# Smaller first transfers, products that warm the array, one wider copy, and a respaced hand-over in an attention and expert kernel

## The chip, the cores and the metric

The kernel runs on one core of a Trainium2 chip. A core has five engines that work at the same time and wait for each other by semaphores: TensorE (PE, matrix products; its weight loads are a row of their own, PEld), VectorE (DVE), ScalarE (ACT), GpSimd (POOL) and SyncE (SP), which issues most transfers. Products are written to PSUM, a small memory in eight banks that PE, DVE and ACT reach; all else lies in SBUF, 128 partitions wide. Sixteen DMA engines carry the data between SBUF and the main memory (HBM). The metric is the time of one execution on the device, in microseconds.

## The reference

Two layers on an image batch `x` of shape (2, 256, 56, 56), seen as 2 × 3136 positions of 256 channels.

```python
# layer 0: a non-local block without softmax, per group of 16 channels
g_x, th_x, ph_x = (einsum('gdc,bcn->bgdn', w, xf) + b for w, b in ...)
f = einsum('bgdn,bgdm->bgnm', th_x, ph_x) / n
y = einsum('bgnm,bgdm->bgdn', f, g_x)
z = relu(batchnorm(w_out @ y + b_out) + x)

# layer 1: causal attention with 4 heads of 64, then 8 experts, two for each token
t = t + attention(layernorm(t))            # t: (2, 3136, 256)
probs = softmax(layernorm(t) @ gate_w + gate_b)
top2_vals, top2_idx = top_k(probs, 2)
out = sum over experts e of  weight_e * (gelu(xf @ w1_e + b1_e) @ w2_e + b2_e)
t = t + out
```

All of it is in float32. As layer 0 has no softmax, the product over positions can be folded: the kernel needs only the 256 × 256 Gram matrix of the rows of `x` and their sums.

## The kernel before, in words

**Layer 0.** The rows of both images are read into `xr` (L187), 128 positions to a row block, four blocks (512 KB) to a transfer, and the tail of 64 (L191). `gram` (L255) accumulates the Gram matrix of an image over 25 row blocks with two products each (257 and 129 columns, since only the upper part is needed). `fold` makes one 256 × 256 matrix of it and of the weights; `apply` (L324) multiplies the image with this matrix, adds, and takes the relu. The gram of the first image is the first work of PE. PE also needs `ident`, an identity matrix that GpSimd makes at the very start. This part is ordered by the scheduler of the language; from layer 1 on the order of the instructions on each engine is that of the program text (`manual_schedule`).

**Attention.** For each image, blocks of W = 448 queries (`i`, 0 to 6) and two pairs of heads (`hp`) run over key blocks of 128 (`j`). One step has three parts. `scores` multiplies keys and queries into a PSUM tile of two banks, one for each head of the pair (L653), ACT takes the exponential into an SBUF tile `st` (L661, five buffers), DVE masks it where it is cut by the diagonal (L663) and adds it to `acc`, from which the row sums come (L675). `values` multiplies `st` with the values three steps later (`LAG`) and accumulates in the PSUM tile `yp` (L693). `yp` has one buffer of two banks; each bank holds the products of one half of the keys of a block, so the result is the sum of the two banks. At the last key block ACT copies bank 0 into the query's place in `qT` (L703), and DVE adds bank 1 to it (L704); only then the first `values` of the next pair may write `yp`. At that first step the next `scores` stand ahead of `values` in PE's queue.

Then follow, spaced by a clock that counts steps (`later`, `due`): `sum_rows` (L720 to L731: row sums by PE, a copy by ACT, four small transfers to HBM and one back in another layout), `invert` (L740 to L746: the reciprocal on DVE, a transfer to HBM, two broadcasts back into `rb`), `scale` (L752: DVE multiplies `qT` with `rb`) and `hand_on`, which marks the queries as finished. `queue_of` sends the transfers of the very last pair through GpSimd's queue, all others through SyncE's.

**Work in between.** Between the steps run generators that are pulled piece by piece from a deque `queue`; a pull takes the first generator in it that has something to do (the value `True`), and goes on to the next where it says `False`. `tokens(b)` holds the output projection (L602, `project_out`, where `finished` allows it), the sort of tokens by expert (`dispatch`: many small DVE instructions and two PE products) and the scatter of rows to their slots in HBM, `x_slots` (L1284, GpSimd). For image 0 all of this takes place during the attention of image 1; at its end the rows of the first three expert blocks are read into `early_rows` (L1659). For image 1 it takes place among the expert blocks.

**Experts.** `experts` runs over 102 blocks `n` of 128 slots each (the loop begins at n = −1). A block has `hidden` (L1403), `inputs` and `weights` of the block two ahead (transposes L1380; a DVE copy of the expert's weights, L1391), `outputs` of the block three back (L1422; DVE adds the bias, L1432; written to `y_slots`, L1437), and then `between()`, which is `meanwhile`: it pulls two pieces, or three while the rows of image 1 are scattered. Rows come in groups of three blocks by `fetch` (L1329); group 0 is `early_rows`. At the front of `queue` stands `closing`: while the last pair of image 1 isn't finished, it moves the clock by 4, calls `due`, and yields twice, so one of `sum_rows`, `invert`, `scale` and `hand_on` comes with each block. Once `hand_on` has run, `tokens(1)` goes on with the last projections, the sort and the scatter. At last come the gathers of the outputs, the sums and the stores (`finish`).

Of the kernel before, what the change touches and what calls it, by code (L numbers as in the profile page):

```python
# [9 lines left out]
F32 = mybir.dt.float32  # L10
# [3 lines left out]
ALU = mybir.AluOpType  # L14
# [13 lines left out]
def conv_attn_moe_kernel(  # L28
# [51 lines left out]
    nc = tc.nc  # L80
    P = 128
    B, C, N = x.shape
# [21 lines left out]
    MIXED = MOST0 + E  # L104
    NBLK = (2 * B * N + E * (P - 1)) // P
    GB = 3

    MAIN = NBLK - GB
    SCALE = 1.0 / HS**0.5
# [63 lines left out]
    with tc.tile_pool(name="c_w", bufs=1) as cw, tc.tile_pool(name="c_s", bufs=2) as cs, tc.tile_pool(  # L173
# [9 lines left out]
        whole = N // P  # L183
        for b in range(B):
            nc.gpsimd.memset(xr[b][:, :, C : C + 1], 1.0)
            for n in range(0, whole, 4):
                nc.sync.dma_start(  # L187
                    out=xr[b][:, n : n + 4, :C],
                    in_=x_rows[b, n * P : (n + 4) * P].rearrange("(n p) c -> p n c", p=P),
                )  # L190
            nc.sync.dma_start(out=xr[b][: N - whole * P, whole, :C], in_=x_rows[b, whole * P :])  # L191
        for b in range(B):
# [124 lines left out]
        def apply(b, meanwhile):  # L317
# [22 lines left out]
                    waiting = n + m  # L340
            nc.sync.dma_start(out=kept[b], in_=ts[b][:, :, :C])

        folded = {}
        first = fold(0, gram(0, iter(())))
        second = fold(1, gram(1, first))
# [97 lines left out]
    def layer1(nm, general):  # L443

        with ExitStack() as whole:
# [170 lines left out]
            def attend(  # L616
# [63 lines left out]
                def values(n):  # L680
                    i, hp, j, first, last, order = steps[n]
                    k = chunk(j)
                    c0 = max(0, j * P - i * W)
                    sn = f"{nm}{b}_{hp}_{i}"
                    st = sts.pop(n)
                    if first:
                        yps[hp, i] = py.tile([P, 2, 512], F32, tag="y", name=f"yp_{sn}")
                    yp = yps[hp, i]

                    for h in range(0, k, HS):  # L690
                        end = last or (h and all(chunk(o) <= h for o in order[order.index(j) + 1 :]))
                        for a in range(2):
                            nc.tensor.matmul(  # L693
                                yp[a * HS : (a + 1) * HS, h // HS, c0:W],
                                v[hp][h : h + HS, j, a, :HS],
                                st[h : h + HS, a, c0:],
                                start=first,
                                stop=bool(end),
                            )
                    if last:  # L700

                        yh = qT[:, hp, i * W : (i + 1) * W]
                        nc.scalar.copy(yh, yp[:, 0, :W])  # L703
                        nc.vector.tensor_tensor(yh, yh, yp[:, 1, :W], ALU.add)  # L704
                        del yps[hp, i]
                        later.append((clock[0], sum_rows, hp, i, yh))

                def queue_of(hp, i):

                    return nc.gpsimd if (b, hp, i) == (B - 1, NH - 1, NB - 1) else nc.sync  # L710

                def sum_rows(hp, i, yh):
                    r = (b * NH + hp) * NB + i
                    sn = f"{nm}{b}_{hp}_{i}"
                    acc = accs.pop((hp, i))
                    sp = bank(f"sp_{b}_{hp}_{i}")

                    flat = acc.rearrange("p a w -> p (a w)")
                    for g in range(4):
                        nc.tensor.matmul(  # L720
                            sp[g * 32 : (g + 1) * 32, : W // 2], ones[:, :32],
                            flat[:, g * W // 2 : (g + 1) * W // 2], start=True, stop=True,
                        )
                    line = fs.tile([P, W], F32, tag="rb", bufs=3, name=f"line_{sn}")
                    nc.scalar.copy(line[:, : W // 2], sp[:, : W // 2])
                    halves = sum_d[r].rearrange("a (h w) -> (a h) w", h=2)
                    for g in range(4):
                        queue_of(hp, i).dma_start(
                            out=halves[g : g + 1], in_=line[g * 32 : g * 32 + 1, : W // 2]
                        )  # L730
                    queue_of(hp, i).dma_start(  # L731
                        out=sums[:, r], in_=sum_d[r].rearrange("a (p f) -> (a p) f", p=HS)
                    )
                    later.append((clock[0] + 4, invert, hp, i, yh))

                def invert(hp, i, yh):
                    r = (b * NH + hp) * NB + i
                    sn = f"{nm}{b}_{hp}_{i}"
                    back = fs.tile([P, 2 * W // P], F32, tag="back", name=f"back_{sn}")
                    nc.vector.reciprocal(back, sums[:, r])  # L740
                    queue_of(hp, i).dma_start(
                        out=inv_d[r].rearrange("a (p f) -> (a p) f", p=HS), in_=back
                    )
                    rb = fs.tile([P, W], F32, tag="rb", bufs=3, name=f"rb_{sn}")
                    for a in range(2):
                        queue_of(hp, i).dma_start(  # L746
                            out=rb[a * HS : (a + 1) * HS], in_=inv_d[r, a].partition_broadcast(HS)
                        )
                    later.append((clock[0] + 4, lambda hp, i, yh: scale(hp, i, yh, rb), hp, i, yh))
# [551 lines left out]
            def experts(w1s, w2s, b2s, ex, es, ps6, between, need, written):  # L1301
# [4 lines left out]
                def fetch(g):  # L1306
                    s, e = g * GB, (g + 1) * GB
                    b = 0 if e <= FULL0 else 1
                    need(b)
                    if g == 0:  # L1310
                        return early_rows, None
                    f = known[b][0]
                    xb = ex.tile([P, GB, xds[b].shape[1]], F32, tag="xb", bufs=3, name=f"xb_{nm}_{g}")
                    if b:
# [59 lines left out]
                def inputs(n, group):  # L1374
                    xb, to = group
                    g = n % GB
                    rows = xb[g] if n < GB else xb[:, g, :C]
                    tp = ps6.tile([P, 512], F32, tag="tp", bufs=2, name=f"tp_{nm}_{n}")
                    for c in range(NH):
                        nc.tensor.transpose(  # L1380
# [257 lines left out]
            def tokens(b, qT, done):  # L1638
# [5 lines left out]
                if b == 0:  # L1644
# [8 lines left out]

                    while not read[B - 1]:
                        yield False
                    for n in range(0, GB, 2):
                        m = min(2, GB - n)
                        xb = bg.tile([P, 2, C], F32, tag="xn", name=f"xb_{nm}_first{n}")
                        nc.sync.dma_start(  # L1659
                            out=xb[:, :m],  # L1660
                            in_=xds[0][n * P : (n + m) * P].rearrange("(n p) w -> p n w", p=P),
# [108 lines left out]
            def closing():  # L1770

                if not general:
                    while finished[B - 1][NH - 1] < N:
                        clock[0] += 4
                        due(clock[0])
                        yield True
                        yield True
                    while not projected[B - 1]:
                        yield False
                    queue.append(judge())  # L1780
# [5 lines left out]
            with ExitStack() as moe:  # L1786
# [11 lines left out]
                        )  # L1798
                for _ in load_w2(True):
                    pass  # L1800
                while len(early_rows) < GB:
                    pull()

                def need(b):
# [9 lines left out]
                    queue.appendleft(finish(1, oy, 3))  # L1814

                def meanwhile():
                    scatters = placed[1] and not sent[1]
                    pull(3 if scatters or worked[0] >= MIXED else 2)
                    if side and next(side[0], None) is None:
                        side.popleft()  # L1820

# [179 lines left out]
```

## Time and profile before

The median of three runs is 1307.98 us (1307.3 to 1308.54). The profiled execution took 1332.96 us, with a span of 1331.2 us and a mean clock of PE of 0.989.

| | us |
|---|---|
| first product of PE (rows of the first image) | 6.19 |
| gram of image 0 done (copy out of PSUM) | 25.66 |
| attention, image 0 and 1 | 110.7 to 886.4 |
| first expert block | 888.2 |
| last projections of image 1 (L602) | 904.0 to 915.8 |
| sort of image 1 (L970 to L1138) | 921.2 to 963.1 |
| scatter of image 1 (L1284) | to 1042.6 |
| last store issued | 1323.9 |

| engine | busy, us | share |
|---|---|---|
| PE | 1276.9 | 96% |
| PEld | 808.0 | 61% |
| DVE | 787.7 | 59% |
| ACT | 602.2 | 45% |
| POOL | 306.2 | 23% |

How to read the rows of the profile below: a row of waits has the engine and line that waited, what ended the wait, then the total in us, the number of times and the longest. A row of the timeline has the start and the length in us, the engine, the line, the operation, what is written and read, the shape, the number of instructions merged in it, and in brackets the idle time of the engine ahead of it with what ended it. A row of a stretch has its bounds, its length, then busy time and number of instructions of PE, PEld, DVE, ACT and POOL, the clock granted to PE, the mean share of the DMA engines, and GB/s. A product in float32 shows as two records.

### The profile page before, as it was taken

The numbers are of one execution on the slowest core, as the hardware profiler recorded it, in microseconds if no ns is written. First come the engines' busy times: TensorE is split into PE (matmuls) and PEld (weight loads), VectorE is DVE, ScalarE is ACT, GpSimd is POOL, SyncE is SP. The second block draws the span as 40 slices with busy tenths as digits, with TensorE's granted clock in tenths as the row PEclk, the third lists the DMA queues.
The fourth block names the chain that finished last, engine by engine and source line by source line (L and its number), as shares of the span: only waits on it lengthen the run. The fifth ranks groups of instructions, "written<-read, shape, count | busy, mean of one in ns | idle before, by whom it ended". The sixth has DMA issues, their size and how long they took to land.

```text
span 1331.2 us, 28014 instructions
## 1 busy us (share of the span) xinstructions
PE 1276.9 (96%) x10569; PEld 808.0 (61%) x10569; DVE 787.7 (59%) x1683; ACT 602.2 (45%) x1226; POOL 306.2 (23%) x297
## 2 busy tenths in 40 slices
PE   8999999999999999999999989989999999899995
PEld 7875444444444444444345434449988999899894
DVE  1582555748777654675768777765744443355553
ACT  0145554555565554455553455553423333244341
POOL 1113110000000111110004461010066212655541
PEclk9999999999999999999999999999999999999997
DMA  9993000000000000100001126141244433556553
GB/s 311 383 326 113 16 24 24 24 16 24 9 17 17 17 2 9 40 9 15 9 8 60 60 80 198 33 138 56 67 144 129 130 109 97 179 175 202 180 156 107
DMA packets 110471, 123.54 MB, mean 93 GB/s; under 512 B 19904, under 2 KB 100045, under 8 KB 110329
## 3 DMA queue, kind: packets, MB, share of 16 engines
q1 hardware_dynamic: 96232, 92.49, 22.4%
q0 software_dynamic: 10272, 26.00, 5.8%
q10 hardware_dynamic: 3824, 3.18, 0.8%
q8 instruction: 87, 1.43, 0.5%
q14 instruction: 56, 0.45, 0.1%
HBM read 62.65 MB, written 60.41 MB: 92 GB/s over the span
## 4 chain that ended last, share of the span: by engine, by line
PE 91%; DVE 3%; issue 2%; ACT 1%; DMA 1%; POOL 0%; DVEq 0%; SPq 0%; POOLq 0%; ACTq 0%
PE yp_f L693 20%; PE sc_f L653 19%; PE ht_f L1403 14%; PE yp_f L1422 13%; PE qk_f L539 7%; PE v_f L558 4%; PE pp_f L602 4%; PE cp L324 3%; PE gram L255 3%; PE tp_f L1380 2%; DVE acc_f L675 1%; ACT st_f L661 1%; PE sp_f L720 1%; PE yo_f L1549 1%; PE xp_f L518 1%
## 5 line engine op out<-in xcount | busy, mean ns | idle before, releaser
L661 ACT ACTIVATE st_f<-sc_f 128x896 f32<-128x896 f32 (+5 forms) x400 | 333.5, 838 | 300.1 <-PE sc_f L653 273.7
L675 DVE TENSOR_TENSOR acc_f<-acc_f,st_f 128x896 f32<-128x896 f32 (+5 forms) x372 | 366.5, 985 | 168.3 <-ACT st_f L661 161.3
L693 PE MATMUL yp_f<-st_f,v_f 64*64 64x448 f32 (+6 forms) x3184 | 340.5, 503 | 9.7 <-DVE qT_f L704 6.5
L653 PE MATMUL sc_f<-qT_f,kT_f 64*64 64x448 f32 (+6 forms) x3184 | 341.5, 500 | 4.0 <-ACT st_f L661 4.0
L1412 ACT ACTIVATE g_f<-ht_f,b1b 128x128 f32<-128x128 f32 x408 | 116.8, 371 | 243.0 <-PE ht_f L1403 127.6
L1403 PE MATMUL ht_f<-xT_f,w_f 128*128 128x128 f32 x1632 | 203.4, 277 | 9.3 <-issue 6.6
L653 PEld LDWEIGHTS sc_f<-qT_f,kT_f 64*64 64x64 f32 x3184 | 116.6, 133 | 156.4 <-issue 134.5
L693 PEld LDWEIGHTS yp_f<-st_f,v_f 64*64 64x64 f32 x3184 | 112.3, 133 | 162.6 <-issue 134.7
L1403 PEld LDWEIGHTS ht_f<-xT_f,w_f 128*128 128x128 f32 x1632 | 198.5, 193 | 14.9 <-issue 10.4
L501 POOL TENSOR_SCALAR xn_f<-t 128x256 f32<-128x256 f32 (+1 forms) x50 | 68.2, 1373 | 542.6 <-issue 330.8
L1284 POOL DMA_INDIRECT x_slots<-xr_f,idx x100 | 113.0, 1130 | 218.7 <-DVE xr_f L1276 116.6
L1391 DVE COPY w_f<-w1s_f 128x1024 f32 x102 | 71.1, 698 | 86.8 <-PE ht_f L1403 38.8
L539 PE MATMUL qk_f<-px_f,wat 128*128 128x512 f32 (+1 forms) x224 | 92.6, 558 | 1.2 <-ACT px_f L524 1.2
L1439 POOL DMA_INDIRECT y_tokens<-ys_f,to_f x60 | 60.3, 1005 | 139.7 <-DVE ys_f L1432 109.8
L1432 DVE TENSOR_TENSOR ys_f<-yp_f,kT_f 128x128 f32<-128x128 f32 x102 | 29.6, 291 | 99.7 <-PE yp_f L1422 65.3
L663 DVE TENSOR_TENSOR st_f<-st_f,keep 128x256 f32<-128x256 f32 (+1 forms) x112 | 44.2, 395 | 68.2 <-ACT st_f L661 67.7
L539 PEld LDWEIGHTS qk_f<-px_f,wat 128*128 128x128 f32 x224 | 38.7, 190 | 54.4 <-issue 45.3
L1422 PE MATMUL yp_f<-px_f,g_f 128*128 x204 | 62.7, 390 | 1.0 <-issue 1.0
L1422 PE MATMUL yp_f<-v_f,g_f 128*128 x204 | 61.5, 382 | 0.8 <-issue 0.8
L1422 PE MATMUL yp_f<-kT_f,g_f 128*128 x204 | 62.1, 386 | 0.0
L1422 PE MATMUL yp_f<-w2s_f,g_f 128*128 x204 | 61.2, 382 | 0.3 <-issue 0.3
L1496 POOL DMA_INDIRECT y_f<-y_slots,idx x50 | 54.8, 1096 | 16.3 <-issue 14.7
(259 smaller groups left out, 1170.8 us busy)
## 6 DMA issues: line engine op xcount, KB each, us to landing
x_slots<-fill SPq DMA_DIRECT2D x1, 8127.0 KB
xb_f<-x_slots SPq DMA_DIRECT2D x60, 129.0 KB
x_slots<-fill SPq DMA_DIRECT2D x1, 7296.0 KB
y_slots<-ys_f SPq DMA_DIRECT2D x57, 128.0 KB
kept<-t SPq DMA_DIRECT2D x2, 3200.0 KB
x<-in_x_dram SPq DMA_DIRECT2D x14, 448.0 KB
xr<-in_x_rows_dram SPq DMA_DIRECT2D x12, 512.0 KB
out_dram<-ot_f SPq DMA_DIRECT2D x24, 256.0 KB
```

Source lines behind the costliest of these rows:

```text
L501: nc.gpsimd.tensor_scalar(xn[:k, a], ts[b][:k, n + a, :C], ts[b][:k, n + a, MEAN : MEAN + 1], ts[b][:k, n + a, RSTD : RSTD + 1], ALU.subtr ...
L539: nc.tensor.matmul(ps[:, :w], wat[:, c, d0 : d0 + P], xT[:, c, :w], start=(c == 0), stop=(c == NH - 1),)
L653: nc.tensor.matmul(ps[h : h + HS, a, c0:W], kT[hp][rows, j * P + h : j * P + h + HS], qT[rows, hp, q0 + c0 : q0 + W], start=True, stop=True,)
L661: nc.scalar.activation(st[:k, :, c0:], ps[:k, :, c0:W], AF.Exp, scale=SCALE)
L675: nc.vector.tensor_tensor(acc[:k, :, c0:], acc[:k, :, c0:], st[:k, :, c0:], ALU.add)
L693: nc.tensor.matmul(yp[a * HS : (a + 1) * HS, h // HS, c0:W], v[hp][h : h + HS, j, a, :HS], st[h : h + HS, a, c0:], start=first, stop=bool( ...
L1284: s = nc.gpsimd.indirect_dma_start(out=xds[b], out_offset=bass.IndirectOffsetOnAxis(ap=idxs[b][:kk, k, n : n + 1], axis=0), in_=xr[:kk], i ...
L1391: nc.vector.tensor_copy(w, w1s[:, :, bass.ds(e, 1), :].rearrange("p c e h -> p c (e h)"))
L1403: nc.tensor.matmul(ht[:, k, :], w[:, c, k * P : (k + 1) * P], xT[:, c, :], start=(c == 0), stop=(c == NH - 1),)
L1412: nc.scalar.activation(g[:, k, :], ht[:, k, :], AF.Gelu, bias=b1bs[b][:, k, i : i + 1])
L1422: nc.tensor.matmul(yp[:, :C], g[:, k, :], w2s[k][:, bass.ds(e, 1), :].rearrange("p e d -> p (e d)"), start=(k == 0), stop=(k == KH - 1),)
L1439: s = nc.gpsimd.indirect_dma_start(out=y_tokens, out_offset=bass.IndirectOffsetOnAxis(ap=to[:, n % GB : n % GB + 1], axis=0), in_=ys, in_o ...
```

## The change

Six edits, each at a place where the kernel goes from one stage to the next.

- The first four row blocks of image 0 come in transfers of one, one and two blocks, so that the first is small.
- Fourteen products of the identity with itself, whose result nobody reads, stand ahead of the gram on PE: they keep the array at work while the rows are on their way.
- At the end of a pair, ACT copies both banks of `yp` in one instruction into a tile from the score buffers, and GpSimd adds the halves: `yp` is free after one copy.
- The last row sums go through SyncE's queue like the others (`queue_of` goes).
- The rows of the first six expert blocks, two groups, are read early.
- `closing` gives six and then four pieces of room after its first two steps, then none; and three pieces are pulled in each block from the end of the projections of image 1 on, not only from the scatter on.

```diff
+    EARLY = 2
...
-            for n in range(0, whole, 4):
+            starts = [0] * (b > 0) + [0, 1, 2] * (b == 0) + list(range(4, whole, 4)) + [whole]
+            for n, end in zip(starts, starts[1:]):
...
+        idle = cbig.tile([P, P], F32, tag="big", name="idle")
+        for _ in range(14):
+            nc.tensor.matmul(idle, ident, ident, start=True, stop=True)
         folded = {}
         first = fold(0, gram(0, iter(())))
...
-                        nc.scalar.copy(yh, yp[:, 0, :W])
-                        nc.vector.tensor_tensor(yh, yh, yp[:, 1, :W], ALU.add)
+                        both = fst.tile([P, 2, W], F32, tag="st", name=f"both_{sn}")
+                        nc.scalar.copy(both, yp[:, :, :W])
+                        nc.gpsimd.tensor_tensor(yh, both[:, 0], both[:, 1], ALU.add)
...
-                    return nc.gpsimd if (b, hp, i) == (B - 1, NH - 1, NB - 1) else nc.sync
...
-                        queue_of(hp, i).dma_start(
+                        nc.sync.dma_start(
...
-                    if g == 0:
-                        return early_rows, None
+                    if g < EARLY:
+                        return early_rows[s:e], None
...
-                    rows = xb[g] if n < GB else xb[:, g, :C]
+                    rows = xb[g] if n < EARLY * GB else xb[:, g, :C]
...
-                    for n in range(0, GB, 2):
-                        m = min(2, GB - n)
-                        xb = bg.tile([P, 2, C], F32, tag="xn", name=f"xb_{nm}_first{n}")
+                    for n, m in ((0, 2), (2, 2), (4, 1), (5, 1)):
+                        name = f"xb_{nm}_first{n}"
+                        if m == 2:
+                            xb = bg.tile([P, 2, C], F32, tag="xn", name=name)
+                        else:
+                            xb = bg.tile([P, C], F32, tag="xr", name=name).unsqueeze(1)
...
+                    blocks = deque((3, 2))
                     while finished[B - 1][NH - 1] < N:
                         clock[0] += 4
                         due(clock[0])
-                        yield True
-                        yield True
+                        for _ in range(2 * blocks.popleft() if blocks else 0):
+                            yield True
...
-                while len(early_rows) < GB:
+                while len(early_rows) < EARLY * GB:
...
-                    scatters = placed[1] and not sent[1]
-                    pull(3 if scatters or worked[0] >= MIXED else 2)
+                    sorting = projected[1] and not sent[1]
+                    pull(3 if sorting or worked[0] >= MIXED else 2)
```

## The prediction

> **What bounds the kernel now.** I began with the chain that ended last and the waits of TensorE (PE), then looked at the three places the change touches.
>
> ```profile
> PE 91%; DVE 3%; issue 2%; ACT 1%; DMA 1%; POOL 0%; DVEq 0%; SPq 0%; POOLq 0%; ACTq 0%
> ```
>
> The end is set by PE: 91% of the chain is PE, which is busy for 1276.9 of 1331.2 us. An edit can shorten the kernel only by taking away time in which PE waits or runs slowly, and costs something only where it makes PE wait.
>
> The start, PE alone, in three stretches (busy time and number of PE products, then loads, DVE, ACT, POOL, clock, DMA share, GB/s):
>
> ```profile
> PE gram L255 <- DMA xr<-in_x_rows_dram: 6.2, 1, 6.2
> ...
> 6.10:12.00 5.90, 5.81 (x18) 4.99 (x19) 0.65 (x2) 0.90 (x1) 0.00 (x0) 1.00 1.03 350
> 12.00:18.00 6.00, 6.00 (x38) 5.49 (x37) 3.03 (x4) 0.89 (x2) 0.00 (x0) 1.00 1.10 336
> ```
>
> The first product waits 6.2 us for rows. Then PE does 18 products in 5.9 us, and 38 in the next 6.0: half speed at first, although the clock column reads 1.00 (single starts show it too: a 129-column product follows the one before after 0.215 us until 11.9 us, after 0.110 us from then on).
>
> PE's waits in attention, and one of them in order of time:
>
> ```profile
> PE yp_f L693 <- DVE qT_f L704: 6.5, 6, 1.5
> PE sc_f L653 <- ACT st_f L661: 4.0, 3, 1.5
> PE yp_f L693 <- issue: 1.4, 1, 1.4
> ...
> 197.25 0.53 ACT L703 COPY qT_f<-yp_f 128x448 f32<-128x448 f32 x1
> ...
> 198.39 0.62 DVE L752 TENSOR_TENSOR qT_f<-qT_f,rb_f 128x448 f32<-128x448 f32 x1
> 198.92 0.61 DVE L704 TENSOR_TENSOR qT_f<-qT_f,yp_f 128x448 f32<-128x448 f32 x1
> ...
> 199.59 0.21 PEld L693 LDWEIGHTS yp_f<-st_f,v_f 64*64 64x64 f32 x8 [1.80 <-DVE qT_f L704]
> 199.59 0.98 PE L693 MATMUL yp_f<-st_f,v_f 64*64 64x448 f32 x8 [1.02 <-DVE qT_f L704]
> ```
>
> The value tile has one buffer. It is free only when DVE has added the second bank (L704), and DVE takes that add after other work: ACT's copy was done at 197.78, the add began at 198.92. Seven of the 27 hand-overs hold PE so, for 6.5 + 1.4 = 7.9 us (the one marked "issue" is at 778.8, where the add ended at 778.76).
>
> The passage from attention to the experts:
>
> ```profile
> DVE back_f L740 <- DMA sums<-sums: 6.5, 1, 6.5
> DVE qT_f L752 <- DMA rb_f<-inverses: 5.2, 1, 5.2
> ...
> PE ht_f L1403 <- DVE w_f L1391: 2.7, 1, 2.7
> PE tp_f L1380 <- DMA xb_f<-x_slots: 1.1, 1, 1.1
> ...
> 893.20:898.50 5.30, 2.41 (x20) 2.21 (x20) 0.88 (x2) 2.04 (x8) 1.07 (x2) 1.00 0.09 21
> 898.50:905.50 7.00, 6.96 (x33) 6.46 (x34) 1.93 (x4) 1.41 (x5) 1.14 (x3) 0.76 0.10 33
> ```
>
> Block 3's rows come 1.1 us late. Then the reciprocal of the last row sums (L740) stands 6.5 us at the head of DVE's queue; the weight copy behind it (L1391) is late, and PE waits 2.7 us for it. Afterwards the clock is 0.76 for 7 us.
>
> **What the Trainium skill says.** *TensorE: Matmul & The Clock Gate*, Part 1: the array starts at half clock and is let go after a busy window of about 3.4 us; the window runs freely, so it takes 3.4 to 6.8 us. The trace agrees (5.7 us). *SBUF — State Buffer*, "Who interferes with whom": a DVE instruction with two SBUF inputs contends with a GpSimd one that reads SBUF; the trace before has no such pair that I could time. *GPSIMD Engine Reference*, 3.1: a two-input add of 2048 fp32 takes 4497 ns, used below.
>
> **Start: small transfers and idle products.** The identity is ready at 1.80 us. Each fp32 product shows as two records, so 14 products are 28. At half speed a record of this size takes 0.215 us, at full 0.110. Starting at 1.9 and let go after 5.7 us, as in this trace, at 7.6, PE has done 26.5 records; the rest takes 0.2, so gram begins at 7.8 at full speed. A block of rows then costs 0.657 us (0.220 + 0.216 + 0.110 + 0.111), 25 of them 16.4: gram ends at 24.2 instead of 25.6, a gain of 1.4. Bounds: let go after 3.4 us, gram starts at 6.6 and ends at 23.1 (gain 2.5); after 6.8, the idle products end at 7.9, gram's first 0.8 us are slow, and it ends at 24.7 (gain 0.9). The rows must keep up: by the packets of their queue the second to fifth transfers of 512 KB had landed by 8.5, 11.3, 13.6 and 16.1 us; the moved gram wants them at 10.4, 13.0, 15.7 and 18.3 (four blocks, 2.6 us, each), so there are 1.7 us in hand. But a transfer waits for the completion of one issued some eight earlier (the third issue stood until 5.78, for a weight load), so small transfers use up places. I take **1.4**, from 0.3 to 2.5. The transfers alone would be worth more than they show here, as PE is held by the idle products until 7.8 anyway.
>
> **One copy for both value banks.** It removes the DVE add from the release (27 × 0.62 us of DVE) and makes the copy 896 columns wide. The exponential of 128x896 takes 0.918 us; of 128x512 0.597, a copy of 128x512 0.586; so the copy should take about 0.91, which is 0.38 more for ACT (45% busy). The tile is then free 0.97 us after the copy's start. For the seven waits I compare this with when PE would have gone on, 0.37 us after its last group of score products: 131.13 against 130.82 and 516.52 against 516.22 leave 0.3 each; 198.22 against 198.40, 586.80 against 586.99, and the three others leave nothing. Gain 7.9 − 0.6 = **7.3**, from 5 to 7.9. The longer copy delays the next exponential by 0.38; its values are wanted three steps of about 1.5 us later, so no PE wait.
> The add moves to GpSimd. By the skill's price it takes 448/2048 × 4497 = 0.98 us (an estimate); by the nearest row (L501, 128x256 in 1.37 us) 2.4. I take 1.5. It is wanted only at L752, after a round trip through memory; but it holds one of the five score buffers, which the exponential four steps (6 us) later takes. Ahead of it in GpSimd's queue stand at most two or three scatters of 1.13 us: 3.4 + 2.4 = 5.8 us at worst. Cost 0.
>
> **The passage.** The early rows of blocks 3 to 5 are read during attention, which takes out the 1.1 us wait; group 2's fetch is due only at block 6. The last sums go through SyncE: earlier ones took 854.12 to 856.23 for the four rows, and inverses to broadcast 861.86 to 864.21, so 2 to 2.4 us a leg; on GpSimd the four issues took 2.6, and the landing another 3.8 us. Spacing counts most: each block pulls two pieces of work, so the reciprocal moves from block 0 to block 2 and the scaling from block 1 to block 4. Sums leave ACT at 888.7, so they are back at about 893.5, behind 1 MB of weights; DVE reaches the reciprocal at about 895. Inverses leave at 895.5, are back by 900.5, and DVE reaches the scaling after block 4's hidden products, about 901. Neither should stand at the head of DVE for long. Behind them on DVE are the weight copies, which PE wants two blocks later. Gain: 1.1 + 2.7 + 7.0 × 0.24 = 5.5 us, from which I take off 0.4 for a short rest of a wait: **5.1**, from 2 to 5.5. SyncE queues the writes of the expert outputs behind these waits; the first is needed only three blocks later.
> One cost I can't see: the new tile lies in memory that expert tiles take over, so the first weight copy may wait for GpSimd's add, between 0 and 1.7 us. I take 0.3.
>
> **Three pieces a block while sorting.** DVE was busy 30.6 of 43 us from 921 to 964; 14.6 of that is weights and outputs, 16 sorting. Half as much more sorting per block makes 3.4 of 3.73 us. Full, but the weight copies have two blocks in hand. Cost 0, and no gain: PE has no wait where the sort's result is first needed, near 1043 us.
>
> **Sum.** 1.4 + 7.3 + 5.1 − 0.3 = 13.5 us, so 1307.98 − 13.5 = **1294.5**. (The profiled execution is 23 us longer than the timed ones; PE waits marked "issue" near 995, 1023, 1144 and 1164 may be part of this. The waits counted here have a releaser in the program, so I carry them over in full.)
>
> **Rivals.**
> B, *the waits in attention come back*: a longer ACT copy or a late GpSimd add holds exponentials up, and nothing of the 7.3 remains: 1308 − 6.2 = 1301.8. For it: PE already waits 4.0 us for exponentials (L653). Against: these are three waits only, and ACT has half its time free.
> C, *the passage's wait only moves*: the scaling stands on DVE for its broadcast at block 4, or the tile taken over delays block 0: of 5.1 some 1.5 stays: 1308 − 1.4 − 7.3 − 1.5 = 1297.8. For it: three legs in memory lie in four short blocks.
> D, *slower*: GpSimd and DVE contend for SBUF and a score buffer comes free late, at each of 27 ends by 0.45 us (12 us), while the fuller DVE makes the passage no better: 1308 − 1.4 + 12 = 1318.6. For it: DVE's main work here (L675) reads two SBUF operands; DVE's lag is what held PE before. Against: 17 us leave DVE.
>
> **Chances.** Forecast 0.60, B 0.15, C 0.15, D 0.10. Faster by over 0.2% takes in the first three, less a little for a mixture near zero: 0.87; same 0.03; slower 0.10. Range: the most of every gain is 2.5 + 7.9 + 5.5 = 15.9, and DVE's freed time may take a few smaller waits along: low 1289. Upward it takes in C and B: high 1303.
>
> **What the next profile shows.** Right: gram's products at one pace from about 7.8 us; the waits of L693 gone or under 1 us; clock near 1 at 890 to 910, no long DVE wait at L740. Wrong, if PE waits for exponentials (L653) longer than 4 us in all, if exponentials wait for GpSimd, or if PE waits for L1391 again.

## The result, and the profile after

The changed kernel takes **1302.59 us** (median of 4 runs, 1302.21 to 1305.95), the kernel before 1308.26 (4 runs, 1307.3 to 1309.54): a ratio of 0.9962, with an interval of 0.9943 to 0.998. So it is faster, by 5.7 us where 13.5 were forecast.

In the first profile of before, from which the prediction was made, and in e1 to e4, e14, e15 and the runs of before beside them, the experts took some 25 us more whatever the kernel, for a reason that stays open, so sizes are compared in the other runs alone, where before takes 1307 to 1308 us; its profile there is called *before, third profile*. Single profiles scatter by a microsecond or two besides.

The table adds up the span of three profiles, between marks that are the start of an instruction in the trace. The last column is a kernel of the experiments (e16, with the start of before), explained there. Sums can be off by 0.1 through rounding.

| us | before, third profile | after | e16 |
|---|---|---|---|
| to the first score product | 110.4 | 111.1 | 109.3 |
| attention, first to last score product | 768.3 | 764.8 | 760.9 |
| last score product to expert block 10 | 46.3 | 41.8 | 41.8 |
| block 10 to the last store's issue | 372.8 | 375.0 | 374.4 |
| last store's issue to the end | 7.5 | 8.2 | 8.6 |
| span | 1305.3 | 1301.0 | 1295.0 |

The gain of after lies in attention (3.5) and in the passage (4.5). The start, the later blocks and the end give 3.6 back. The chain that ended last is still PE's; its share fell from 91% to 88%:

```profile
PE 88%; DVE 3%; issue 2%; DMA 2%; ACT 2%; POOL 2%; DVEq 0%; POOLq 0%; SPq 0%; ACTq 0%
```

POOL, at 0% before, now has 2%, and the next views show where. (DMA has 2% in the third profile of before too.)

**The start.** The two largest waits of PE in the first 30 us, after:

```profile
PE idle L349 <- POOL ident masks.py:199: 1.9, 1, 1.9
PE gram L258 <- DMA xr<-in_x_rows_dram: 1.9, 1, 1.9
```

And two stretches of it, all engines (first pair: PE's busy time and products):

```profile
6.10:12.00 5.90, 5.90 (x39) 5.51 (x39) 0.26 (x2) 0.00 (x0) 0.00 (x0) 1.00 1.04 364
12.00:18.00 6.00, 4.14 (x26) 3.61 (x26) 3.42 (x5) 1.79 (x2) 0.00 (x0) 1.00 1.11 335
```

Before, PE did 18 products in the first of these stretches and 38 in the second; now 39 and 26, of which ten are idle products. By 18 us the gram is no further than before (53 of its records begun, 54 before). The array is warm when the rows come (the gram begins at 7.3 us, at full pace), but it then overtakes them: from 12.5 to 14.6 us it waits for the transfer that holds row blocks 8 to 11. The semaphore of that transfer counts sixteen completions; in the trace the first came at 11.3 us and the last at 14.6.

**Attention.** The largest waits of PE in attention, first before (third profile, 110 to 879 us), then after (110 to 876 us):

```profile
PE yp_f L693 <- DVE qT_f L704: 7.9, 7, 1.5
```

```profile
PE xp_f L525 <- POOL xn_f L508: 2.2, 2, 1.2
PE yp_f L700 <- DVE st_f L670: 1.5, 3, 1.1
PE sc_f L660 <- ACT st_f L668: 0.9, 2, 0.6
PE yp_f L700 <- ACT both_f L711: 0.9, 2, 0.4
```

The wait for DVE's add of the second bank is gone, and 0.9 us for the wide copy is what remains of it. New at the top stands a wait for rows that GpSimd normalises. Its place, first on POOL, then on PE:

```profile
447.38 1.25 POOL L712 TENSOR_TENSOR qT_f<-both_f 128x448 f32<-128x448 f32 x1 [39.14 <-ACT both_f L711]
448.61 8.88 POOL L508 TENSOR_SCALAR xn_f<-t 128x256 f32<-128x256 f32 x6
```

```profile
453.69 0.44 PE L525 MATMUL xp_f<-ident,xn_f 128*128 128x128 f32 x2 [1.16 <-POOL xn_f L508]
455.13 0.44 PE L525 MATMUL xp_f<-ident,xn_f 128*128 128x128 f32 x2 [1.01 <-POOL xn_f L508]
```

GpSimd stood for 39 us at the add of a pair (L712), whose banks were not there yet. The normalisations of image 1's first rows (L508) are behind it in the queue and start only at 448.61; PE then takes the rows as fast as they are made, 1.4 us apiece. The experiments show when GpSimd made them otherwise.

A second place is near 778 us, while GpSimd also scatters rows (all engines, the lines that matter):

```profile
776.52 0.97 POOL L1288 DMA_INDIRECT x_slots<-xr_f,idx  x1 [0.30 <-issue]
...
776.89 3.93 DVE L682 TENSOR_TENSOR acc_f<-acc_f,st_f 128x896 f32<-128x896 f32 x2
...
777.51 1.15 POOL L712 TENSOR_TENSOR qT_f<-both_f 128x448 f32<-128x448 f32 x1
...
778.70 1.73 ACT L668 ACTIVATE st_f<-sc_f 128x896 f32<-128x896 f32 x2 [3.20 <-POOL qT_f L712]
...
779.66 0.98 PE L660 MATMUL sc_f<-qT_f,kT_f 64*64 64x448 f32 x8 [0.65 <-ACT st_f L668]
```

The banks had been copied by 773.41. Three scatters go first, the add begins at 777.51, the exponential that follows it at 778.70 (ACT had been free for it from 775.50, 2.1 us after the copy), and PE's score products wait 0.65 us. The first of DVE's two adds (L682) beside it took 2.73 us instead of 1.09.

**The passage.** Stretches of the kernel after; PE's clock is the third number from the end:

```profile
888.00:893.50 5.50, 5.50 (x41) 5.19 (x40) 1.97 (x4) 2.58 (x10) 0.00 (x0) 1.00 0.43 125
893.50:900.50 7.00, 7.00 (x42) 6.23 (x41) 4.03 (x12) 1.86 (x7) 0.00 (x0) 1.00 0.09 29
```

The clock is 1.00 in both, where before had 0.76 in the second. PE has no wait in either: 41 products in the first 5.5 us, where before had 20 in 5.3. On DVE the reciprocal and the scaling no longer hold anything up:

```profile
887.42 0.20 DVE L744 RECIPROCAL back_f<-sums 128x7 f32<-128x7 f32 x1
...
894.90 0.62 DVE L756 TENSOR_TENSOR qT_f<-qT_f,rb_f 128x448 f32<-128x448 f32 x1
```

Neither has an idle time in brackets; before they stood 6.5 and 5.2 us at the head of DVE.

### The profile page after: what moved, and what is told of

The parts are those of the page before. It is cut to its first block, busy times and chain, and to the rows that moved or that the text cites. A ratio compares the mean times of both kernels' runs of the same rounds, so it can differ in the third digit from the quotient of the medians.

```text
span 1301.0 us, 28091 instructions
## 1 busy us (share of the span) xinstructions
PE 1269.3 (98%) x10597; PEld 806.6 (62%) x10597; DVE 792.0 (61%) x1655; ACT 610.7 (47%) x1226; POOL 343.6 (26%) x317
## 4 chain that ended last, share of the span: by engine, by line
PE 88%; DVE 3%; issue 2%; DMA 2%; ACT 2%; POOL 2%; DVEq 0%; POOLq 0%; SPq 0%; ACTq 0%
PE yp_f L700 20%; PE sc_f L660 19%; PE ht_f L1407 13%; PE yp_f L1426 12%; PE qk_f L546 7%; PE v_f L565 4%; PE pp_f L609 3%; PE cp L327 3%; PE gram L258 2%; PE tp_f L1384 2%; DMA xr<-in_x_rows_dram 1%; PE sp_f L724 1%; DMA y_tokens<-ys_f,to_f 1%; ACT st_f L668 1%; PE yo_f L1553 1%
## 5 line engine op out<-in xcount | busy, mean ns | idle before, releaser
L682 DVE TENSOR_TENSOR acc_f<-acc_f,st_f 128x896 f32<-128x896 f32 (+5 forms) x372 | 375.2, 1009 | 156.3 <-ACT st_f L668 147.3
L1407 PE MATMUL ht_f<-xT_f,w_f 128*128 128x128 f32 x1632 | 199.5, 275 | 0.6 <-ACT xT_f L1388 0.6
L712 POOL TENSOR_TENSOR qT_f<-both_f 128x448 f32<-128x448 f32 x28 | 36.3, 1296 | 522.7 <-ACT both_f L711 522.7
L508 POOL TENSOR_SCALAR xn_f<-t 128x256 f32<-128x256 f32 (+1 forms) x50 | 72.9, 1466 | 143.1 <-DVE t L171 48.7
L546 PEld LDWEIGHTS qk_f<-px_f,wat 128*128 128x128 f32 x224 | 38.7, 190 | 54.0 <-issue 43.6
```

The costliest lines, as they stand in the source:

```text
L508: nc.gpsimd.tensor_scalar(xn[:k, a], ts[b][:k, n + a, :C], ts[b][:k, n + a, MEAN : MEAN + 1], ts[b][:k, n + a, RSTD : RSTD + 1], ALU.subtr ...
L546: nc.tensor.matmul(ps[:, :w], wat[:, c, d0 : d0 + P], xT[:, c, :w], start=(c == 0), stop=(c == NH - 1),)
L682: nc.vector.tensor_tensor(acc[:k, :, c0:], acc[:k, :, c0:], st[:k, :, c0:], ALU.add)
L1407: nc.tensor.matmul(ht[:, k, :], w[:, c, k * P : (k + 1) * P], xT[:, c, :], start=(c == 0), stop=(c == NH - 1),)
```

## The experiments

Times are medians; each ratio is to before, measured beside the kernel. Line numbers shift by a few from kernel to kernel; the tile names stay. Parts are named as in the prediction: *start* (small transfers and idle products), *copy* (one copy, the add on GpSimd), *passage* (SyncE for the last sums, six early blocks, spaced pieces, fuller sorting).

**The parts one by one: e1 to e4.** The kernel before once more, and before with one part each.

```diff
# e2: one copy for both banks
-                        nc.scalar.copy(yh, yp[:, 0, :W])
-                        nc.vector.tensor_tensor(yh, yh, yp[:, 1, :W], ALU.add)
+                        both = fst.tile([P, 2, W], F32, tag="st", name=f"both_{sn}")
+                        nc.scalar.copy(both, yp[:, :, :W])
+                        nc.gpsimd.tensor_tensor(yh, both[:, 0], both[:, 1], ALU.add)
# e3: the passage alone
+    EARLY = 2
...
+                    blocks = deque((3, 2))
...
+                    sorting = projected[1] and not sent[1]
# e4: the start alone
+        for _ in range(14):
+            nc.tensor.matmul(idle, ident, ident, start=True, stop=True)
```

> The kernel before, unchanged. Its first profile had a span of 1331.2 us beside timed runs near 1308. Theory P (that profile is of an unusual execution): a second profile has a span near 1306, lacks the waits of TensorE marked issue near 993 to 1025 and 1143 to 1166 (18 us), and some of the waits in attention are smaller too. Theory R (a profile always makes this kernel 23 us slower): the second span is again near 1330. Time the same as before, within 0.1% under both.

> Of the change, only the one copy for both value banks with GpSimd's add. By the prediction's term it gains 7.3 us (seven waits of 7.9 us go, 0.6 stays): 1301.0. Rival: in timed executions these waits are smaller than in the first profile, and the gain is 2 to 4 us: 1304 to 1306.

> Of the change, only the passage from attention to the experts: six early row blocks, the last sums through SyncE, the spaced closing, three pieces a block from the end of the projections. By the prediction's term it gains 5.1 us: 1303.2; the waits of TensorE at the first expert blocks (1.1 and 2.7 us) and the low clock after them go. Rival: part of the gain is given back later, and it gains 2 us or less: 1306 or more.

> Of the change, only the small first transfers and the fourteen products of the identity. Prediction's term: a gain of 1.4 us, 1306.9. Theory S, from the profile after: the third transfer of four blocks is issued late, the gram waits 2 us for it, and there is no gain (0 to 0.6 us slower): 1308.3 to 1308.9.

Before took 1333.73 us beside these (51 runs). e1: 1335.4, ratio 1.0006 (0.9987 to 1.0024); e2: 1331.37, 0.9985 (0.997 to 1.0001); e3: 1334.59, 1.0013 (0.9997 to 1.0029); e4: 1334.95, 1.0008 (0.9991 to 1.0026). **Inconclusive**, because of what stands in the profile of e1 among the experts (two of the waits of PE from 905 us on, then a stretch of 100 us):

```profile
PE ht_f L1403 <- issue: 6.7, 9, 1.1
PE yp_f L1422 <- issue: 2.3, 4, 1.0
```

```profile
950.00:1050.00 100.00, 93.79 (x603) 85.48 (x603) 49.03 (x188) 32.05 (x115) 52.16 (x50) 0.95 0.41 129
```

The same stretch in the third profile of before:

```profile
950.00:1050.00 100.00, 100.00 (x695) 93.28 (x694) 55.07 (x195) 36.72 (x131) 53.47 (x50) 1.00 0.43 141
```

PE does 603 products instead of 695: it waits up to 1.1 us for nothing that the profile shows, and the mean clock of the stretch is 0.95. All four profiles here have such waits at L1403 and its like, before and its parts alike, so the kernel's edits don't make them; what does is open. The prediction left open whether such waits are part of the 23 us between profile and times. They are. They also swallow gains: in e3 block 5 began at 901.1 us, 8.5 earlier than in e1 (909.6), yet the ends differ by 2.7.

**Two mends, beside the changed kernel: e5 to e8.** e6 leaves the small transfers out and keeps the idle products; e7 puts the add on VectorE; e8 does both.

```diff
# e6, e8
-            starts = [0] * (b > 0) + [0, 1, 2] * (b == 0) + list(range(4, whole, 4)) + [whole]
-            for n, end in zip(starts, starts[1:]):
+            for n in range(0, whole, 4):
# e7, e8
-                        nc.gpsimd.tensor_tensor(yh, both[:, 0], both[:, 1], ALU.add)
+                        nc.vector.tensor_tensor(yh, both[:, 0], both[:, 1], ALU.add)
```

> The changed kernel, unchanged. In its first profile TensorE has no waits marked issue among the experts, while four other profiles (the kernel before and parts of the change) have 17 to 22 us of them, in stretches where products come in pairs 0.71 us apart. Theory H (these belong to the chip or the execution, not to the kernel): on a chip where the kernel before takes about 1333, this one has them too, and takes 1322 to 1330; on a chip where the kernel before takes about 1308, it takes about 1302.6 without them. Theory K (the change itself removes them): it takes 1301 to 1306 wherever it runs.

> The changed kernel with the first rows in transfers of 512 KB as before; the idle products stay. Theory S (the small transfers use up places in the queue, so that the third transfer of four blocks is late and the gram stands 2.1 us): the wait goes, the gram of image 0 ends about 2 us earlier (near 24.2 us), and the time is 1.5 to 2 us under that of the changed kernel. Rival: without the small transfers the first product waits for rows as long, and there is no difference.

> The changed kernel with the add of the two halves on VectorE, from the copied tile, instead of on GpSimd. Theory G (the add stops GpSimd at each pair's end, and the normalisations of image 1's first rows, which it did hundreds of us ahead before, come only when TensorE needs them, 2.7 us of waits near 454): these waits go, and the time is 2 to 3 us under that of the changed kernel. Rival: VectorE's 17 us more of work bring other waits back, no difference or slower.

> Both mends: transfers of 512 KB and the add on VectorE. If theories S and G hold and add up, 4 to 5 us under the changed kernel.

Before: 1308.07 (11 runs). e5: 1302.89, 0.9969 (0.9957 to 0.9981). e6: 1302.03, 0.9954 (0.994 to 0.9967). e7: 1300.84, **0.9942** (0.9928 to 0.9956). e8: 1299.81, 0.9947 (0.9934 to 0.9961).

The small first transfers are probably part of what makes the gram wait, but not all of it. With large ones (e6) PE waits 1.8 us for rows, with small ones 1.9 (after); in e8, also large, 0.5. By the semaphore counts in the traces, the whole transfer with row blocks 8 to 11 had landed at 14.2 to 14.6 us in all four kernels with small transfers (after, e4, e5, e7), and at 12.5 to 13.4 in all with large ones but e6, where it came at 14.1. So it can be late without them too. The times with large transfers are 0.9 and 1.0 us lower (e6 under e5, e8 under e7), less than the 1.5 to 2 of theory S and within the intervals, so its number is neither shown nor refuted. Its reason falls: with small transfers this one was issued at 4.6 to 5.2 us, and with large ones no sooner (5.1 to 5.8). Why it lands later isn't shown. None of the four gram ends (26.2 after, 25.7, 26.1, 24.5 in e6, e7, e8) is earlier than the earliest of the old start (24.2).

The add's engine matters: e7 is 2 us under e5, as theory G has it. In e7, POOL's normalisations (all between 270 and 458 us) and then PE at the place shown above:

```profile
285.21 2.87 POOL L508 TENSOR_SCALAR xn_f<-t 128x256 f32<-128x256 f32 x2 [44.91 <-PE xp_f L525]
...
452.39 5.15 POOL L508 TENSOR_SCALAR xn_f<-t 128x256 f32<-128x256 f32 x4 [164.32 <-issue]
```

```profile
451.57 1.09 PE L525 MATMUL xp_f<-ident,xn_f 128*128 128x128 f32 x8
```

GpSimd has made the first two row blocks at 285 us, 166 us ahead, and was idle since; PE transposes both in one go at 451.57, without a wait. Before does the same (third profile):

```profile
287.14 2.88 POOL L501 TENSOR_SCALAR xn_f<-t 128x256 f32<-128x256 f32 x2 [44.95 <-PE xp_f L518]
```

In after the two stand in the queue behind five adds, at 315, 342, 377, 407 and 447 us, and so come last. Attention takes 760.7 us in e7 against 768.3 before: 7.6 less, where 7.3 were forecast. The scatter is small here: 764.8 to 765.0 in the three profiles with the adds on GpSimd (after, e5, e6), 760.7 in both with them on VectorE (e7, e8). e8 is 3.1 us under e5, not the 4 to 5 of both mends, since the start gave less than S said.

**The parts again where the waits "issue" are away: e9 to e11.** Same kernels as e1 to e3.

> The kernel before, unchanged, for a profile of it on a chip where it takes 1308 us (both of its profiles so far are of executions near 1333). If this is such a chip, theory W (its waits in attention and at the passage are there as in the first profiles) expects 7 to 9 us of waits of TensorE for the add of the second bank and 4 us at the first expert blocks, and a span near 1306 without the waits marked issue; theory V (on such a chip these waits are smaller) expects 5 us less of them in all, which would be the part of the forecast gain that is missing.

> The copy part alone once more, beside the kernel before on the same chip. Where the kernel before takes 1308: theory W with the found wait for the normalisations, 7.9 - 0.6 - 2.7 = 4.6 us, 1303.5; theory V: 2 us or less.

> The passage alone once more, beside the kernel before on the same chip. Where the kernel before takes 1308: theory W 4.5 to 5.1 us, 1303.2; theory V: 2 us or less, 1306 or more.

e9, a single run of before: 1307.03, with a span of 1305.3 us and no waits marked issue at the hidden or output products: so the first profile was the unusual one (theory P of e1), and theory R falls. Its waits are 7.9 us for the add of the second bank and 3.4 us (2.7 and 0.7) at the first expert blocks, close to what theory W says; V falls, and the missing gain must have another cause. e10: 1305.82, **0.9988** (0.9981 to 0.9994). e11: 1304.38, **0.9978** (0.9971 to 0.9986). By its time e10 fits V (2 us or less) and e11 lies between W and V, but V's reason, smaller waits, is gone. In e10 attention shrank by 0.6 us only. PE's wait for L501 is there as in after, and here it took the clock along (e10):

```profile
450.00:455.00 5.00, 2.84 (x16) 1.25 (x18) 1.60 (x2) 1.89 (x3) 5.00 (x5) 0.75 0.00 0
455.00:460.00 5.00, 5.00 (x29) 1.53 (x22) 1.20 (x2) 1.11 (x2) 2.85 (x3) 0.56 0.00 0
```

From score product 800 to 1592, which spans this place, e10 takes 174.0 us, after 171.0, before and e7 168.3. In e11 last scores to block 10 take 41.0 us instead of 46.3, a gain of 5.4, of which the time shows 2.7. So half of it is lost later.

**What the start is worth, and what gives the passage's gain back: e12 and e13.** e12 is e7 with the start of before. e13 is e11 with the sorting at two pieces a block:

```diff
-                    sorting = projected[1] and not sent[1]
-                    pull(3 if sorting or worked[0] >= MIXED else 2)
+                    scatters = placed[1] and not sent[1]
+                    pull(3 if scatters or worked[0] >= MIXED else 2)
```

> Kernel after with the add on VectorE, and with the start of before (transfers of four blocks, no idle products). Theory F (the warm start is worth nothing, because the array then waits for rows): gram of image 0 ends within 0.7 us of before, 24.2 to 25.5 us, and the time is that of the same kernel with the new start, 1300 to 1301 us where before takes 1307 to 1308: a ratio of 0.994 to 0.9955. Rival W (the warm start is worth the 1.4 us of the forecast, and the measured starts only hide it by their scatter): 1.4 us more than with the new start, about 1302, a ratio of 0.9955 to 0.9965.

> Kernel before with the passage's edits alone (early rows, SyncE for the last sums, spaced pieces), but the sorting still with two pieces a block. Theory K (the fuller sorting is what gives back part of the gain: the store of image 1 that waits for VectorE in blocks 60 to 70, and the longer tail after the last store): the lead over before at block 10, 5.5 to 6 us, is kept, last store to end takes 7.3 to 7.7 us, and the time is 5 us under before, ratio about 0.996. Rival T (the sorting has no part in it; the tail is a matter of queues on SyncE and GpSimd that every shift of the experts meets): as with the fuller sorting, 2.5 to 3 us under before, ratio 0.9975 to 0.998, tail of 8 to 9 us.

Before: 1308.2 (11 runs). e12: 1300.31, 0.994 (0.9926 to 0.9953); with the new start (e7) it was 0.9942. The times alone could hide 1.4 us, as each interval reaches 1.8 us to either side. The profiles settle it: with the old start (13 profiles) the gram ended at 24.2 to 25.8 us, 24.9 on the mean, and the first score product came at 109.8 on the mean; with the new one (six profiles) at 24.5 to 26.2, mean 25.7, and at 110.6. The new start gains nothing and rather costs 0.8 us: theory F stands, W falls. e13: 1304.31, 0.9971 (0.996 to 0.9982), not told from e11: it lies between the forecasts of K and T, and the interval takes in both. Its profile divides the loss. Block 10 to block 60 takes 190.0 us in before and e13, 190.4 in e11: 0.4 for the fuller sorting. Blocks 60 to 70 take 38.7 before, but 39.5 in e13 and 39.7 in e11. There image 1's outputs are summed; in block 68 PE waits for them, 0.8 us in after and 0.6 in e11 and e13, and not in before. (e5, the same kernel as after, has no such wait and takes 38.7.) All waits of this kind, most of them behind the last block, before (third profile) and after:

```profile
PE yo_f L1549 <- DVE y_f L1536: 7.0, 3, 4.6
```

```profile
PE yo_f L1553 <- DVE y_f L1540: 8.3, 5, 5.1
```

The tail is 8.7 us in e13 as well, as theory T says. Theory K explains 0.4 us; the rest comes with the passage's other edits, and T's reason for it (queues) isn't shown. SyncE's waits after the last products, before (third profile) and after:

```profile
SPq L1937 <- SPq L1937: 2.7, 1, 2.7
```

```profile
SPq L1946 <- SPq L1946: 4.8, 2, 2.8
```

The line is the branch behind layer 1 (`tc.If(n_done < P)`). SyncE pauses there once in the six profiles without the passage's edits, and a second time, for 1.8 to 2.2 us, in all thirteen with them. What makes the second pause isn't shown: no wait of the program stands there.

**A new wait, and its mend: e14 to e17.** e12 gains 7.5 us in attention, but from the last scores to block 10 it takes 44.5 us, not after's 41.8. Its longest wait of PE at 870 to 895, and a stretch:

```profile
PE ht_f L1401 <- DVE w_f L1389: 1.9, 1, 1.9
```

```profile
876.70:880.20 3.50, 3.45 (x17) 3.48 (x18) 0.50 (x1) 0.30 (x1) 0.00 (x0) 0.53 0.32 104
```

With all adds on DVE the last one stands ahead of the first weight copies of the experts; PE waits 1.9 us, and the clock is 0.53 for the next 3.5 us. e14 is e12 with that one add on GpSimd; e15 also takes the fuller sorting out. Both were run twice, as before took 1335 us beside the first pair (e14, e15) and 1308 beside the second (e16, e17).

```diff
-                        nc.vector.tensor_tensor(yh, both[:, 0], both[:, 1], ALU.add)
+                        eng = nc.gpsimd if (b, hp, i) == (B - 1, NH - 1, NB - 1) else nc.vector
+                        eng.tensor_tensor(yh, both[:, 0], both[:, 1], ALU.add)
```

> As the kernel with VectorE adds and the old start (1300.3 us, profile 1298.7), but the add of the very last pair is on GpSimd. Theory V (with all adds on VectorE the first weight copies of the experts come 1.9 us late, because they stand behind the last add, and the clock then falls for 3.4 us): the wait of block 0 for L1389 goes, block 0 follows the last score products after 3.9 to 4.1 us instead of 5.8, block 10 after 41 to 42 us instead of 44.4, and the time is some 2.5 us less, 1297.5 to 1298.5, a ratio of 0.9915 to 0.993. Rival U (the weight copies are late for another reason, their own transfers): block 0 after 5.5 to 6 us, ratio 0.994 as before.

> The same with the sorting at two pieces a block. If the fuller sorting gives back 0.7 us in blocks 60 to 70 (as the single profiles say), 0.3 to 1 us less than with the fuller sorting; if not, the same within 0.3. In either case the tail from the last store to the end stays at 8 to 9 us, since the passage's other edits are in.

> The kernel of the run with the last add on GpSimd once more, because there the kernel before took 1335 us, 27 more than where the other parts were measured. Where before takes 1307 to 1308: theory V gives 1297.5 to 1298.5 (ratio 0.9915 to 0.993), theory U 1300.3 (0.994).

> The same with the sorting at two pieces a block. If the fuller sorting gives back 0.7 us: 0.3 to 1 us under the run beside it. If, as beside the kernel before at 1335, it is worth 3 us: 1294.5 to 1295.5.

e14: 1331.48 beside 1335.06, 0.9975 (0.9964 to 0.9987); e15: 1328.25, 0.9948 (0.9928 to 0.9968). e16: **1298.28** beside 1307.86, 0.9935 (0.9922 to 0.9949). e17: **1297.53**, 0.9921 (0.9908 to 0.9935), the fastest kernel here, 10.3 us under before. In e16 the only wait of PE over 0.2 us at the experts up to 900 us is:

```profile
PE ht_f L1402 <- ACT xT_f L1383: 0.6, 1, 0.6
```

The wait for the weight copy is gone, block 0 follows the last scores after 3.9 us (5.9 in e12), and block 10 after 41.8: by the profile theory V stands and U falls. The ratio, 0.9935, lies between their forecasts and would not tell them apart. e17 ends with e16 in the profile (1294.9 and 1295.0), and the intervals overlap, so of the sorting I only say that two pieces a block are no worse; the 3 us between e14 and e15 were not seen again. (e14 has the waits marked issue among the experts as well, so theory K of e5, by which the change removes them, falls.)

## Why the prediction was right or wrong

The direction held; 13.5 us were forecast and 5.7 came. The range held by a little luck, at its upper end of 1303, which rivals B and C had set. In the profiles of the table 4.3 us came of 13.5. Of the 9.2 that are missing, 3.8 are the copy's, 2.9 are lost in later blocks and at the end, 2.1 are the start's and 0.3 the passage's. By its own terms:

**"One copy for both value banks", 7.3: the removal was right, one of its costs was not.** With the adds on VectorE attention shrinks by 7.4 to 7.5 us (e16, e12). The copy took 0.90 us (0.91 forecast). What failed is the sentence "Cost 0" for the add on GpSimd; it costs 4.0 us (764.8 in after against 760.8 in e12). I had counted what stands *ahead* of the add in GpSimd's queue, and who reads its buffer, but not what is queued *behind* it. An instruction that waits for the end of each pair takes away the lead of everything after it in that queue, here the normalisations: 2.7 us at 448 to 455. A further 1.2 us lies between score products 2400 and 2800, where the wait for the add behind three scatters stands. There my bound ("two or three scatters") was right and the slack ("four steps, 6 us") was not: the exponential wanted the buffer 2.1 us after the copy, and the add ended 5.2 us after it. So one of the prediction's signs of being wrong came true, an exponential that waits for GpSimd, once, for 3.2 us. Rival B, with exponentials held up by a late add, is partly what happened, at 0.15; of the 7.3 it left 3.5, not 0. (The 4.0 us of waits for exponentials that spoke for B stood in the first profile only; the third of before has none.) The wait for the normalisations (L501) was in no case.

**"Start", 1.4: nothing, or a loss.** The warm-up is as worked out: full pace came 3.6 to 6.2 us after the first idle product (4.6 in after), against the prediction's estimate of 3.4 to 6.8. The gram began at 7.3 us (7.8 forecast), and from there to its end at 26.2 it took 18.9 us, 16.7 without its waits (16.4 forecast). The mis-sized term is the "1.7 us in hand" for the rows. I had read it from the bytes that the queue had moved. PE went on only when the whole transfer had landed: at 14.6 us in after, where the gram wanted it at 12.5. In the prediction's own profile the whole had landed at 12.5 and not at 11.3, so 1.2 us of the 1.7 were never there; the other 2 us of the delay are new in after, and their cause stays open (e6). The warm array turned slow products into a wait for data. The base was off too: the profile whose 25.6 us the gain was counted from has the latest gram end of the 13 with the old start. In these the slow pace lasted anything from 3.0 to 6.0 us after the first product, and one profile (5.7) was taken for all.

**"The passage", 5.1 − 0.3: right.** 4.5 us in after, 5.4 alone (e11). Block 3's rows, the sums at the head of DVE and the low clock are all gone, by the steps told, and the tile taken over shows no wait. What remains is 0.6 us for ACT at block 2. Rival C, by which the wait only moves, didn't happen: neither the reciprocal nor the scaling stands on DVE. Its four edits were run together only, so which of them gives how much isn't shown.

**What had no term: the gain is carried to the end in full.** 2.9 us come back: 2.2 from block 10 to the last store and 0.7 after it. Every kernel with the passage's edits loses there, e5 1.6 us, e13 2.0, e16 2.7, e11 3.3; e10, without them, 0.1. Shown are the places (1.3 us in blocks 60 to 70, with 0.8 us of waits of PE for the sums of image 1, and SyncE's second pause at the end); why they come with an earlier start of the experts isn't settled.

The sum of these in the profile: −0.7 + 3.5 + 4.5 − 2.2 − 0.7 = 4.4 us (4.3 by the spans). The times show 5.7 and, in e5, 5.2.

**Sorting, 0:** 0.4 us in the profiles, below what the times tell apart. **Rival D** (slower): its mechanism is real but small. DVE's adds beside GpSimd's:

```profile
L682 DVE TENSOR_TENSOR acc_f<-acc_f,st_f 128x896 f32<-128x896 f32 (+5 forms) x372 | 375.2, 1009 | 156.3 <-ACT st_f L668 147.3
```

They take 375.2 us against 366.5 in the third profile of before and 366.6 in e12. That is 8.7 us of DVE for 28 adds of GpSimd, 0.3 each, and DVE has that time free.

## What to carry to other kernels

Before an instruction that waits for another engine is moved to an idle engine, list what stands behind it in that engine's queue: what used to run far ahead will now run just in time. A warm array helps only if the data are there, so compare when a *whole* transfer lands with when it is wanted, at the new pace. And take a gain at a hand-over in full only up to the next wait that the trace shows; past that, find out which transfers the earlier start now meets.

## What the runs showed of the hardware

- GpSimd's two-input add of 128x448 from SBUF took 1.30 us on the mean of 28. The estimate from the Trainium skill's *GPSIMD Engine Reference*, 3.1, was 0.98; the 1.5 taken was nearer.
- The Trainium skill's *SBUF — State Buffer*, "Who interferes with whom", says that such a pair of DVE and GpSimd instructions contends for a shared port. The trace agrees, with a size: of 37 full DVE adds that ran into a GpSimd add, 20 took their usual 1.09 us and 17 took 1.31 to 2.73: eleven 0.33 us longer, two 0.22, two 0.65, two 1.6. The prediction said that the trace before had no such pair to time. It had: 20 full adds ran beside a normalisation on GpSimd, and three of them took 1.19 to 1.24 us.
- The sixteen completions of one 512 KB transfer of rows (blocks 8 to 11) came within 1.1 us in the first profile of before (11.4 to 12.5) and within 3.3 us in after (11.3 to 14.6).
- With the same start the array ran at the slow pace for 3.0 to 6.0 us from its first product, in 13 profiles.
- A wait of PE is followed by a low clock in some cases and not in others. After 1.9 us (e12, at 876.7) the clock was 0.53 for 3.5 us; after the two waits of 1.0 and 1.2 us near 454, it stayed 1.00 in after and fell to 0.56 in e10.
